# Selective scans in a two-layer MetaFormer: row sums at a unit's start, roots on GpSimd, whole-row products

## The chip, the cores and the metric

The kernel runs on one core of a Trainium2 chip. The metric is the device time of one execution in microseconds (us). Five engines work side by side, each through its own queue in order: PE (TensorE, matrix products), DVE (VectorE), ACT (ScalarE), POOL (GpSimd) and SP (SyncE, which here only issues transfers). They wait for one another by semaphores. SBUF is the on-chip memory of 128 partitions; PSUM holds the results of PE.

## The reference, cut to what matters

Two layers, each a mixing part and a feed-forward part with residuals, on x of shape (4, 256, 32, 32). The change lies in layer 1: its mixer is a selective scan in four directions, its feed-forward a router that sends each token to two of eight experts.

```python
def _selective_scan(x, A_log, D, W_delta, b_delta, W_B, W_C):
    delta = jax.nn.softplus(x @ W_delta + b_delta)
    Bm = x @ W_B
    Cm = x @ W_C
    A = -jnp.exp(A_log)
    dA = jnp.exp(delta[..., None] * A)
    dBx = (delta * x)[..., None] * Bm[:, :, None, :]
    def combine(left, right):
        a_l, b_l = left
        a_r, b_r = right
        return (a_l * a_r, a_r * b_l + b_r)
    _, h = jax.lax.associative_scan(combine, (dA, dBx), axis=1)
    y = jnp.einsum('blcn,bln->blc', h, Cm) + x * D
    return y
...
out1 = corr(flat)
out2 = jnp.flip(corr(jnp.flip(flat, axis=1)), axis=1)
rows = features.transpose(0, 2, 3, 1)
rows_f = jnp.flip(rows, axis=1).reshape(B, H * W, C)
out3 = jnp.flip(corr(rows_f).reshape(B, H, W, C), axis=1).reshape(B, H * W, C)
cols = features.transpose(0, 3, 2, 1)
cols_f = jnp.flip(cols, axis=1).reshape(B, W * H, C)
out4 = jnp.flip(corr(cols_f).reshape(B, W, H, C), axis=1)
...
mamba_out = (out1 + out2 + out3 + out4) / 4
...
# layer 1
x = x + _L1_conv_ref(_ln_c(x), ...)
t = _to_tokens(x)
t = t + _L1_ffn_ref(_ln_t(t), ...)   # normalizes again, then top 2 of 8 experts
```

Both norms before the experts divide by a root: `_ln_t` by sqrt(var + 1e-5), and the feed-forward's own by the root of the variance that is left, again with 1e-5.

## The kernel before

**Stages.** Layer 0 (attention with a top-k, its experts) takes the first 2190 us. Then the scan stage, 2192 to 3391 us, is written out by hand: instructions go to each engine's queue in the order in which the Python code issues them (`tc.manual_schedule()`). After it come the experts of layer 1 in 36 tiles of 256 slots, where a scheduler orders the instructions (the tail).

**A turn.** The scan stage has 128 units of work, called turns here: 4 batches b x 2 halves of channels c x 16 states s. Sixteen turns with one (b, c) make a unit. A turn works on tiles of 128 channels by 1024 positions in float32. In `turn(k)`, in this order:

- the generators in `steps` and `complete` are advanced by one step (called A in the prediction);
- PE: `begin()` clears the turn's sum in PSUM with a product of zeros (L2055), `columns_added()` adds the column scan of the turn before (L2095). If a generator uses the idle PSUM sum (`ps_m`), `begin` comes behind `columns_added`;
- ACT: `column_decays()` (da_c, L2033) for the next turn; POOL: `third()` of the turn before, an elementwise product into its da_c (L2084), which PE adds to the sum (L2061);
- PE: `output_added()` of two turns before adds yc to y (L2105);
- ACT: `products(cum)` for the next turn (L2037), from the row sums of delta, which are the same for all 16 turns of a unit;
- DVE: `forth()` (scan, L2066) and `back()` (scan into PSUM, L2073); POOL takes a small difference (gap, L2070); PE adds the forth scan twice (L2061);
- ACT: `decays()` (da, L2041); POOL and ACT: `inputs()` for the next turn (uu, L2049 and L2050); one scatter DMA if one is under way (L1984);
- DVE: `output()` of the turn before: yc = sum * C in two halves (L2101); then `come_in()`, a short scan (L2079);
- the generators are advanced by one more step (B);
- DVE: `cum`, the row sums, at the end of the turn two before a unit's first one (L2202), then `columns()`, the scan over columns (L2090).

So DVE's row in a bare turn is forth, back, yc, yc, come, columns.

**Generators beside the turns.** `Prep.steps` prepares the next batch (its norm, the products for B, C and delta, the softplus); it starts in turn 0 of batch 0's first unit, and in turn 8 of the first unit of batches 1 and 2. Its last pieces (L1861 to L1867), over four half rows, finish delta and dx and add D * x to the residual. `routed(b - 1)` starts in turn 2 of batches 1 to 3: `norm` (mean, transposes, squares on ACT, then two inverse roots) and `route` (best and second-best expert, counts, slots), after which 16 scatters go out, one a turn. For the last batch the same two generators run in the tail beside the experts' first tiles.

**The roots.** `rsqrt` (L1713) takes ACT's square root, which needs another function table than Exp, and refines its reciprocal by five small DVE instructions. `norm` does so twice.

Of the kernel before, what the change touches and what calls it, by code (L numbers as in the profile page):

```python
# [11 lines left out]
F32 = mybir.dt.float32  # L12
# [4 lines left out]
AF = mybir.ActivationFunctionType  # L17
ALU = mybir.AluOpType
# [16 lines left out]
E = 8  # L35
HID = 1024
NF = HID // P
NS = 16
# [24 lines left out]
def metaformer(ctx: ExitStack, tc: tile.TileContext, t: dict, out: bass.AP):  # L63
# [1530 lines left out]
    def route(b, tok, slot, space, psum, tag):  # L1594
# [15 lines left out]
        best(m1, hot1)  # L1610
        yield
        yield
        nc.vector.tensor_scalar(tok[:, :, C + 1], red, -1.0, float(E), ALU.mult, ALU.add)
        nc.vector.tensor_copy(tok[:, :, C], goal[:, ts(b, NT)])
# [63 lines left out]
    def norm(b, tok, pool, psum, tag, raw_tag, d):  # L1678
# [14 lines left out]
        for r in range(NT // 2):  # L1693
# [10 lines left out]
            for i in range(2):  # L1704
# [5 lines left out]
        ve, sd, r0, s1, s2 = (pool.tile([P, NT], F32, tag=f"nm_{i}", name=f"nm_{i}")  # L1710
                              for i in ("ve", "sd", "r0", "s1", "s2"))

        def rsqrt(dst):  # L1713

            yield
            nc.scalar.activation(sd, ve, AF.Sqrt)  # L1716
            yield
            nc.vector.reciprocal(r0, sd)
            nc.vector.tensor_tensor(sd, r0, r0, ALU.mult)
            nc.vector.tensor_tensor(sd, sd, ve, ALU.mult)  # L1720
            nc.vector.tensor_scalar(sd, sd, -0.5, 1.5, ALU.mult, ALU.add)
            nc.vector.tensor_tensor(dst, r0, sd, ALU.mult)

        nc.vector.tensor_scalar(ve, var, 1e-5, None, ALU.add)
        yield from rsqrt(s1)
        nc.vector.tensor_tensor(ve, s1, s1, ALU.mult)
        nc.vector.tensor_tensor(ve, ve, var, ALU.mult)
        nc.vector.tensor_scalar(ve, ve, 1e-5, None, ALU.add)
        nc.vector.tensor_tensor(lg1, lg1, s1.unsqueeze(2).to_broadcast([P, NT, E]), ALU.mult)
        yield from rsqrt(s2)  # L1730
        nc.vector.tensor_tensor(s2, s2, s1, ALU.mult)
# [37 lines left out]
    class Prep:  # L1769
# [7 lines left out]
        def steps(self, room, psum, tag):  # L1777
# [82 lines left out]
            for c, cols in parts:  # L1860
# [79 lines left out]
    with ExitStack() as st:  # L1940
# [21 lines left out]
        beside = [(2, places()), (FIRST, chain(whole(0), preps[0].steps(room, ps_n, "t"), lead.steps(preps[0]))), (SECOND, whole(1))]  # L1962
# [27 lines left out]
    with ExitStack() as st:  # L1990
# [22 lines left out]
        class Scan:  # L2013
# [84 lines left out]
            def output(self):  # L2098
                self.yc = [p2.tile([P, HALF], F32, tag="yc", name="yc", bufs=4) for h in range(NHALF)]
                for h in range(NHALF):  # L2100
                    nc.vector.tensor_tensor(self.yc[h], self.sum[:, ts(h, HALF)], self.cb[:, ts(h, HALF)], ALU.mult)  # L2101

            def output_added(self, y):
                for h in range(NHALF):
                    nc.tensor.matmul(y[:, ts(h, HALF)], ident, self.yc[h], start=(self.s == 0), stop=(self.s == NS - 1))  # L2105
# [31 lines left out]
        def turn(k):  # L2137
# [5 lines left out]
            next(complete, None)  # L2143
            shared = k > 0 and len(ps_m.left) < NHALF
# [20 lines left out]
            if 0 <= k < len(order):  # L2165
# [9 lines left out]
                if b + 1 < B and c * NS + s == (BEHIND if b > 0 else 0):  # L2175
                    steps.append(preps[b + 1].steps(room, ps_m, "hp"))
# [251 lines left out]
```

## Time and profile before

| what | us |
|---|---|
| median of 3 runs | 3993.39 (3991.88 to 3993.66) |
| profiled execution: its time | 3987.99 |
| profiled execution: its span | 3986.0 |
| scan stage, first forth to the last turn's end | 2192 to 3391 |
| busy in the span: PE, DVE, ACT, POOL | 3385.9, 3040.6, 2820.0, 1895.9 |
| scans on DVE (L2066, L2073, L2090), x128 each | 2.27 to 2.28 each |
| yc (L2101), x256 | 0.68 each |
| cum (L2202), x7 | 2.27 to 2.28 each |
| table loads for the norm's root (L1716), x8 | 1.28 each |

In the page, a row of engines shows the span in forty slices with the busy share in tenths. On a timeline, each row is a start, a duration, an engine, a source line, the operation, out<-in with shapes, and in brackets how long the engine was idle before it and what ended that. A table of windows gives, for stretches of time, the busy time of each engine, with the number of instructions, then the granted PE clock as a share of full speed, the share of the DMA engines and GB/s. Durations on one engine overlap a little[...].

### The profile page before, as it was taken

Reading aid. Unit: us, or ns where it says so; the run is one execution under the profiler, and the core shown is the slowest. Engines: PE = TensorE matmul, PEld = TensorE weight load, DVE = VectorE, ACT = ScalarE, POOL = GpSimd, SP = SyncE. Lnnn points to the kernel's source line nnn. Section 1 sums busy time; section 2 is a strip of 40 time slices with the busy share of each in tenths; the row PEclk is TensorE's granted clock in tenths of the full one; section 3 lists DMA queues with packets and bytes.
Section 4 is the critical chain, followed back from the end, with each engine's and each line's share of the span. In section 5 each row is a group of like instructions: output and inputs, shape, how many; then the busy total and the mean of one; then the engine's idle time right before and its main releaser. Section 6 shows DMA issues by size and latency. Waiting matters only on the chain. (4 is left out here: it accounts for less than half of the span.)

```text
span 3986.0 us, 49764 instructions
## 1 busy us (share of the span) xinstructions
PE 3385.9 (85%) x17283; PEld 1901.2 (48%) x17330; DVE 3040.6 (76%) x5416; ACT 2820.0 (71%) x3772; POOL 1895.9 (48%) x1643
## 2 busy tenths in 40 slices
PE   8368888888888888886697888988988989999996
PEld 5134444534354444543475333443433433788885
DVE  2689898998989898989476899999999999301112
ACT  2889999899989999996245677867767767322222
POOL 0145544575638475576343756545546546121111
PEclk8577887788778777787798999999999999999997
DMA  9400084000000000000374444334334334665555
GB/s 292 109 1 1 1 232 123 1 1 29 13 1 1 1 33 1 1 12 17 108 236 128 139 121 135 116 100 130 120 100 129 123 104 139 208 191 185 189 194 187
DMA packets 241815, 393.71 MB, mean 99 GB/s; under 512 B 31888, under 2 KB 182160, under 8 KB 241424
## 3 DMA queue, kind: packets, MB, share of 16 engines
q1 hardware_dynamic: 218016, 340.54, 27.7%
q0 software_dynamic: 19904, 48.48, 3.8%
q8 instruction: 139, 2.28, 0.2%
q10 hardware_dynamic: 3632, 1.40, 0.1%
q14 instruction: 124, 1.02, 0.1%
HBM read 280.41 MB, written 109.94 MB: 98 GB/s over the span
## 5 line engine op out<-in xcount | busy, mean ns | idle before, releaser
L823 POOL TENSOR_SCALAR dr<-s_n,last 128x1024 bf16<-128x1024 f32 x250 | 718.9, 2892 | 734.7 <-DVE state L851 407.8
L733 ACT ACTIVATE junk_a<-s_n,state 128x1024 int8<-128x1024 f32 x448 | 514.6, 1149 | 25.3 <-DVE state L857 9.0
L2084 POOL TENSOR_TENSOR da_c<-prod,come 128x1024 f32<-128x1024 f32 x128 | 248.3, 1940 | 444.8 <-DVE h L2090 353.5
L737 DVE TENSOR_SCALAR_CACHE_REDUCE junk_v<-s_n,state 128x1024 int8<-128x1024 f32 x320 | 408.6, 1277 | 8.8
L2276 ACT ACTIVATE hid<-hp,b 128x256 f32<-128x256 f32 x288 | 133.7, 473 | 357.0 <-PE hp L2274 356.8
L784 DVE SCALAR_TENSOR_TENSOR w<-s_n,win 128x1024 f32<-128x1024 f32 x256 | 350.9, 1371 | 5.3
L2095 PE MATMUL sum<-h,ident 128*128 128x512 f32 x512 | 269.1, 651 | 96.2 <-DVE h L2090 91.6
L787 DVE MAX8 win<-w 128x8 f32<-128x1024 f32 x256 | 314.5, 1228 | 8.8
L2073 DVE TENSOR_TENSOR_SCAN sum<-da,uu 128x1024 f32<-128x1024 f32 x127 | 289.7, 2281 | 27.2 <-remote 13.3
L891 ACT ACTIVATE ex<-sT 128x1024 f32<-128x1024 f32 x256 | 246.9, 1016 | 88.1 <-PE sT L883 88.1
L2049 POOL TENSOR_TENSOR uu<-dx,bb 128x1024 f32<-128x1024 f32 x127 | 302.4, 2381 | 1.9 <-DMA bb<-bc_d 1.8
L733 ACT ACTIVATE junk_a<-s_n,guess 128x1024 int8<-128x1024 f32 x256 | 294.2, 1149 | 7.2
L2066 DVE TENSOR_TENSOR_SCAN h<-da,uu 128x1024 f32<-128x1024 f32 x127 | 288.3, 2270 | 1.0 <-POOL uu L2049 1.0
L2090 DVE TENSOR_TENSOR_SCAN h<-da_c,uu 128x1024 f32<-128x1024 f32 x127 | 288.9, 2275 | 0.0
L901 PE MATMUL o_ps<-ex,vT 128*32 128x256 f32 x2048 | 238.5, 449 | 53.9 <-ACT ex L891 39.1
L2285 DVE TENSOR_TENSOR ys<-yp,b2e 128x512 f32<-128x512 f32 x36 | 24.9, 692 | 323.7 <-PE yp L2282 323.7
L2033 ACT ACTIVATE da_c<-delta,a_log 128x1024 f32<-128x1024 f32 x128 | 267.0, 2086 | 5.3 <-DMA rows_y<-ys 5.2
L2061 PE MATMUL sum<-da_c,ident 128*128 128x512 f32 x512 | 252.2, 615 | 16.0 <-POOL da_c L2084 10.3
L2287 POOL DMA_INDIRECT results<-ys,to x72 | 69.8, 969 | 411.8 <-DVE ys L2285 186.6
L2274 PE MATMUL hp<-xe,w 128*128 128x256 f32 x1152 | 260.2, 383 | 6.1 <-DVE xe L2262 5.9
L767 ACT COPY s_n<-sp 128x1024 f32<-128x1024 f32 x256 | 245.3, 1003 | 18.1 <-PE sp L759 10.3
L2282 PE MATMUL yp<-w2e,hid 128*128 128x256 f32 x1152 | 255.9, 379 | 0.0
(681 smaller groups left out, 7557.3 us busy)
## 6 DMA issues: line engine op xcount, KB each, us to landing
cb<-bc_d SPq DMA_DIRECT2D x128, 512.0 KB, 4.1
bb<-bc_d SPq DMA_DIRECT2D x127, 512.0 KB, 4.9
w<-in_w SPq DMA_DIRECT2D x36, 1024.0 KB, 5.1
w2e<-in_w SPq DMA_DIRECT2D x36, 1024.0 KB, 5.5
slots_x<-zeros SPq DMA_DIRECT2D x1, 33669.0 KB
slots_x<-zeros SPq DMA_DIRECT2D x1, 33282.0 KB, 120.9
w<-in_w SPq DMA_DIRECT2D x72, 256.0 KB, 3.1
xs<-slots_x SPq DMA_DIRECT2D x36, 261.0 KB, 3.3
```

Of the source, the lines that this page charges most:

```text
L733: nc.scalar.activation(junk, self.row(r), AF.Sign, bias=thr, scale=-1.0, accum_out=u)
L737: nc.vector.tensor_scalar(junk, self.row(r), thr, None, ALU.is_lt, ALU.add, accum_out=u)
L784: nc.vector.scalar_tensor_tensor(w, self.row(r), self.win[:, r, 0:1], self.row(r), ALU.is_gt if r < LAST_DVE else ALU.is_ge, ALU.subtract, ...
L787: nc.vector.max(out=self.win[:, r, 1:], in_=w)
L823: ins = eng.tensor_scalar(dr, self.row(r), self.last[:, r : r + 1], None, ALU.is_lt)
L2033: nc.scalar.activation(grid(self.da_c), cols_flipped(self.prep.delta[:, self.c]), AF.Exp, scale=self.decay)
L2049: nc.gpsimd.tensor_tensor(self.uu[:, 0], self.prep.dx[:, self.c], self.bb, ALU.mult)
L2066: nc.vector.tensor_tensor_scan(rows.rearrange("p r w -> p (r w)"), self.da, self.uu[:, 0], 0.0, ALU.mult, ALU.add)
L2073: nc.vector.tensor_tensor_scan(self.sum[:, ::-1], self.da[:, ::-1], self.uu[:, 0][:, ::-1], 0.0, ALU.mult, ALU.add)
L2090: nc.vector.tensor_tensor_scan(self.hs, self.da_c, self.uu[:, 1], 0.0, ALU.mult, ALU.add)
L2095: nc.tensor.matmul(cols_flipped(self.sum[:, ts(h, HALF)]), ident, grid(self.hs)[:, :, ts(h, half)], start=False, stop=False)
L2274: nc.tensor.matmul(hp[:, f % 2], self.w1[:, c, ts(f, P)], self.xe[:, c], start=(c == 0), stop=(c == CT - 1))
```

## The change: what it does

Five edits.

- `output()`: yc becomes one instruction over 1024 positions, into one buffer of two instead of two of four; the products that add it to y read its halves.
- `norm`: both inverse roots become a power of -1/2 on POOL, taken once each and not refined; seven small POOL instructions replace fifteen of DVE and two of ACT. The generator has two steps fewer. `minus_half` is a tile that layer 0's router has already.
- `route`: two small DVE writes (the expert's number and the token's goal) move two steps up, right behind the first search.
- `Prep.steps`: with `whole_rows`, the last pieces run over two whole rows of 1024 instead of four halves, so with half as many instructions and steps. The first preparation, which lies in layer 0's end, keeps the halves.
- `turn`: the row sums of a unit are taken in the turn before its first one, behind the A steps and before forth, instead of at the end of the turn before that, in front of `columns()`.

```diff
         best(m1, hot1)
+        nc.vector.tensor_scalar(tok[:, :, C + 1], red, -1.0, float(E), ALU.mult, ALU.add)
+        nc.vector.tensor_copy(tok[:, :, C], goal[:, ts(b, NT)])
         yield
         yield
-        nc.vector.tensor_scalar(tok[:, :, C + 1], red, -1.0, float(E), ALU.mult, ALU.add)
-        nc.vector.tensor_copy(tok[:, :, C], goal[:, ts(b, NT)])
         nc.vector.scalar_tensor_tensor(lg1, hot1, -1e30, lg1, ALU.mult, ALU.add)
...
-        def rsqrt(dst):
-
-            yield
-            nc.scalar.activation(sd, ve, AF.Sqrt)
-            yield
-            nc.vector.reciprocal(r0, sd)
-            nc.vector.tensor_tensor(sd, r0, r0, ALU.mult)
-            nc.vector.tensor_tensor(sd, sd, ve, ALU.mult)
-            nc.vector.tensor_scalar(sd, sd, -0.5, 1.5, ALU.mult, ALU.add)
-            nc.vector.tensor_tensor(dst, r0, sd, ALU.mult)
-
-        nc.vector.tensor_scalar(ve, var, 1e-5, None, ALU.add)
-        yield from rsqrt(s1)
-        nc.vector.tensor_tensor(ve, s1, s1, ALU.mult)
-        nc.vector.tensor_tensor(ve, ve, var, ALU.mult)
-        nc.vector.tensor_scalar(ve, ve, 1e-5, None, ALU.add)
+        nc.gpsimd.tensor_scalar(ve, var, 1e-5, None, ALU.add)
+        nc.gpsimd.tensor_tensor(s1, ve, minus_half, ALU.pow)
+        yield
+        yield
+        nc.gpsimd.tensor_tensor(ve, s1, s1, ALU.mult)
+        nc.gpsimd.tensor_tensor(ve, ve, var, ALU.mult)
+        nc.gpsimd.tensor_scalar(ve, ve, 1e-5, None, ALU.add)
+        nc.gpsimd.tensor_tensor(s2, ve, minus_half, ALU.pow)
+        nc.gpsimd.tensor_tensor(s2, s2, s1, ALU.mult)
         nc.vector.tensor_tensor(lg1, lg1, s1.unsqueeze(2).to_broadcast([P, NT, E]), ALU.mult)
-        yield from rsqrt(s2)
-        nc.vector.tensor_tensor(s2, s2, s1, ALU.mult)
         yield
...
-            for c, cols in parts:
+            for c, cols in [(c, slice(0, L)) for c in range(CT)] if whole_rows else parts:
                 dx = self.dx[:, c, cols]
...
             def output(self):
-                self.yc = [p2.tile([P, HALF], F32, tag="yc", name="yc", bufs=4) for h in range(NHALF)]
-                for h in range(NHALF):
-                    nc.vector.tensor_tensor(self.yc[h], self.sum[:, ts(h, HALF)], self.cb[:, ts(h, HALF)], ALU.mult)
+                self.yc = p2.tile([P, L], F32, tag="yc", name="yc")
+                nc.vector.tensor_tensor(self.yc, self.sum, self.cb, ALU.mult)
...
             next(complete, None)
+            if 0 < k + 1 < len(order) and order[k + 1][2] == 0:
+                b, c, _ = order[k + 1]
+                cum = p1.tile([P, L], F32, tag="cum", name="cum") if cum is lead.cum else lead.cum
+                nc.vector.tensor_tensor_scan(cum, inner, preps[b].delta[:, c], 0.0, ALU.mult, ALU.add)
...
-            if 0 <= k + 2 < len(order) and order[k + 2][2] == 0:
-
-                b, c, _ = order[k + 2]
-                if k < 0:
-                    cum = lead.cum
-                    return
-                cum = p1.tile([P, L], F32, tag="cum", name="cum") if cum is lead.cum else lead.cum
-                nc.vector.tensor_tensor_scan(cum, inner, preps[b].delta[:, c], 0.0, ALU.mult, ALU.add)
+            if k == -2:
+                cum = lead.cum
+                return
```

More of the change, by code (lines that the diff above doesn't have):

```diff
@@ L1709, in norm @@
             yield
-        ve, sd, r0, s1, s2 = (pool.tile([P, NT], F32, tag=f"nm_{i}", name=f"nm_{i}")
-                              for i in ("ve", "sd", "r0", "s1", "s2"))
-        def rsqrt(dst):
-            yield
-            nc.scalar.activation(sd, ve, AF.Sqrt)
-            yield
-            nc.vector.reciprocal(r0, sd)
-            nc.vector.tensor_tensor(sd, r0, r0, ALU.mult)
-            nc.vector.tensor_tensor(sd, sd, ve, ALU.mult)
-            nc.vector.tensor_scalar(sd, sd, -0.5, 1.5, ALU.mult, ALU.add)
-            nc.vector.tensor_tensor(dst, r0, sd, ALU.mult)
-        nc.vector.tensor_scalar(ve, var, 1e-5, None, ALU.add)
-        yield from rsqrt(s1)
-        nc.vector.tensor_tensor(ve, s1, s1, ALU.mult)
-        nc.vector.tensor_tensor(ve, ve, var, ALU.mult)
-        nc.vector.tensor_scalar(ve, ve, 1e-5, None, ALU.add)
+        ve, s1, s2 = (pool.tile([P, NT], F32, tag=f"nm_{i}", name=f"nm_{i}") for i in ("ve", "s1", "s2"))
+        nc.gpsimd.tensor_scalar(ve, var, 1e-5, None, ALU.add)
[7 more added lines that the diff above has]
+        nc.gpsimd.tensor_tensor(s2, s2, s1, ALU.mult)
         nc.vector.tensor_tensor(lg1, lg1, s1.unsqueeze(2).to_broadcast([P, NT, E]), ALU.mult)
-        yield from rsqrt(s2)
-        nc.vector.tensor_tensor(s2, s2, s1, ALU.mult)
         yield
@@ L1775, in __init__, with steps @@
             self.bc = bc_dram.tile([2 * NS, L], F32, tag="bc_d", name="bc_d")
-        def steps(self, room, psum, tag):
+        def steps(self, room, psum, tag, whole_rows):
             b = self.b
@@ L1960, in places @@
                     [P, *shape], F32, tag=f"at{len(shape)}", name="at", bufs=4))
-        beside = [(2, places()), (FIRST, chain(whole(0), preps[0].steps(room, ps_n, "t"), lead.steps(preps[0]))), (SECOND, whole(1))]
+        beside = [(2, places()), (FIRST, chain(whole(0), preps[0].steps(room, ps_n, "t", False), lead.steps(preps[0]))), (SECOND, whole(1))]
         for i in range(USUAL):
@@ L2098, in output @@
             def output(self):
-                self.yc = [p2.tile([P, HALF], F32, tag="yc", name="yc", bufs=4) for h in range(NHALF)]
-                for h in range(NHALF):
-                    nc.vector.tensor_tensor(self.yc[h], self.sum[:, ts(h, HALF)], self.cb[:, ts(h, HALF)], ALU.mult)
+                self.yc = p2.tile([P, L], F32, tag="yc", name="yc")
+                nc.vector.tensor_tensor(self.yc, self.sum, self.cb, ALU.mult)
             def output_added(self, y):
                 for h in range(NHALF):
-                    nc.tensor.matmul(y[:, ts(h, HALF)], ident, self.yc[h], start=(self.s == 0), stop=(self.s == NS - 1))
+                    nc.tensor.matmul(y[:, ts(h, HALF)], ident, self.yc[:, ts(h, HALF)], start=(self.s == 0), stop=(self.s == NS - 1))
             def finish(self, y):
@@ L2175, in turn @@
                 if b + 1 < B and c * NS + s == (BEHIND if b > 0 else 0):
-                    steps.append(preps[b + 1].steps(room, ps_m, "hp"))
+                    steps.append(preps[b + 1].steps(room, ps_m, "hp", True))
                 ys.append(ps_y.tile([P, L], F32, tag="y", name="y") if s == 0 else ys[-1])
```

## The prediction

> **What bounds the kernel now.** I read the page's slices first, then the scan stage (2192 to 3391 us, 128 turns) cut into its eight units of 16 turns, then single turns on the timeline. The columns of the second fence: stretch, its length, and busy time with instruction count of PE, PEld, DVE, ACT, POOL; then clock, DMA.
>
> ```profile
> DVE  2689898998989898989476899999999999301112
> ```
> ```profile
> 2342.00:2492.00 150.00, 128.64 (x305) 53.30 (x312) 145.29 (x116) 104.88 (x71) 96.11 (x63) 0.99 0.42 129
> 2492.00:2642.00 150.00, 138.89 (x391) 64.38 (x395) 139.84 (x163) 114.13 (x107) 69.06 (x46) 0.96 0.34 112
> ```
>
> DVE is full through the scans; a unit with a norm in it (the second row) has more DVE instructions, less DVE busy time and a lower clock. So the stage is DVE's row plus knots in the norm units. After it PE is full (tail, 3392 to 3890 us). One undisturbed turn on DVE:
>
> ```profile
> 3305.58 2.27 DVE L2066 TENSOR_TENSOR_SCAN h<-da,uu 128x1024 f32<-128x1024 f32 x1
> 3307.76 2.28 DVE L2073 TENSOR_TENSOR_SCAN sum<-da,uu 128x1024 f32<-128x1024 f32 x1
> 3309.94 1.27 DVE L2101 TENSOR_TENSOR yc<-sum,cb 128x512 f32<-128x512 f32 x2
> 3311.13 0.22 DVE L2079 TENSOR_TENSOR_SCAN come<-prod,gap 128x32 f32<-128x32 f32 x1
> 3311.26 2.27 DVE L2090 TENSOR_TENSOR_SCAN h<-da_c,uu 128x1024 f32<-128x1024 f32 x1
> ```
>
> Starts follow one another without a hole: 7.86 us a turn (next start 3313.44). What counts is the distance between starts, since ends overlap the next by 0.09 us. The two yc halves take 3309.94 to 3311.13. PE is nearly as full: 7.72 us busy of 7.80 in this turn.
>
> The knots. Before a unit's first scan the row sum (cum, L2202) sits between come and the column scan:
>
> ```profile
> 2792.42 0.60 PE L2055 MATMUL sum<-nought 128*128 128x512 bf16 x2
> 2795.15 3.68 PE L2095 MATMUL sum<-h,ident 128*128 128x512 f32 x4 [2.13 <-DVE h L2090]
> 2798.64 1.91 PE L2061 MATMUL sum<-da_c,ident 128*128 128x512 f32 x4
> ```
> ```profile
> 2800.58 1.29 DVE L2101 TENSOR_TENSOR yc<-sum,cb 128x512 f32<-128x512 f32 x2 [1.12 <-PE sum L2061]
> ```
>
> PE stood idle 2.13 us, its next four matmuls took 3.68 us instead of 1.98, and DVE then waited 1.12 us for the sum: the turn cost 9.09. yc's start also tells that it comes after all four adds of da_c (the last begins at 2799.95 and takes 0.59), not after the first half's two. The turns behind the seven cum scans, in windows (second-last but one number is the clock):
>
> ```profile
> 2488.70:2496.60 7.90, 7.68 (x18) 3.07 (x18) 7.90 (x8) 4.55 (x4) 4.49 (x3) 1.00 0.16 45
> 2795.00:2804.10 9.10, 8.95 (x17) 3.74 (x18) 7.98 (x7) 5.75 (x4) 5.48 (x4) 0.81 0.23 67
> 3102.30:3111.40 9.10, 8.92 (x17) 3.80 (x18) 8.01 (x7) 5.72 (x4) 5.48 (x4) 0.81 0.25 80
> ```
>
> At 2488 a PE gap of 2.35 us left the clock at 1.00: the drop is a matter of chance at gaps of 2 to 2.5 us. For the norm:
>
> ```profile
> 2574.03 1.28 ACT L1716 ACT_TABLE_LOAD   x1
> 2575.32 0.21 ACT L1716 ACTIVATE nm_sd<-nm_ve 128x8 f32<-128x8 f32 x1
> ```
> ```profile
> L304 POOL TENSOR_TENSOR space<-space,minus_half x3: 1670/1675/1683, 838.6 to 1720.2; 128x8 f32<-128x8 f32 x3
> ```
>
> The second is the layer-0 router's root, the operation that the norm will now use: 1.675 us on 128x8. Its neighbours L303 and L305 to L307 take 0.20 each.
>
> **What the Trainium skill says.** "TensorE: Matmul & The Clock Gate", Part 1 (What's actually happening): the clock falls to half after an idle window of about 3.4 us, and that window runs freely. The trace agrees on half rate (four matmuls 0.85 apart instead of 0.43) and on chance, but shows the drop after 2.13 us already. "VectorE: DVE Perf Modes", The TRN2 errata: an instruction pays a fixed cost on top of its elements. Agrees: 0.59 us between starts for 512 elements, 1.11 for 1024 (L2110, 2673.59 to 2674.70). "ScalarE: Activation LUTs", What ACT_TABLE_LOAD costs: 1283 ns; so does the trace. "GPSIMD Engine Reference", Specifications: it shares its SBUF interfaces with VectorE. The DVE scans take 2.27 with POOL's multiply beside them and without, so I charge nothing for POOL's added work.
>
> **The change part by part.** Turns are counted inside a unit, 0 to 15 for one (batch, half of channels); a step of a generator runs at the turn's start (A) or after come, ahead of the column scan (B).
>
> 1. Product with C over the whole row. One instruction of about 1.11 (L2110's distance; same size, one operand in PSUM) for a pair of 1.18: 0.07 x 128 = 9.0 us. Nothing starts later: yc already waits for all four adds. Its reader is the y matmul two turns on; two whole buffers hold what four halves held. If PE binds in the bare turns (7.72 of 7.80) some of it is lost: between -9 and -6. I take -9.0.
>
> 2. Roots on POOL. DVE loses per norm 8 dependent operations (2582.34 to 2583.84, 1.50 us), 6 more (2593.05 to 2594.15, 1.10) and L1724 (0.06): 2.66, three norms 8.0. One part is given back: with 1.5 us less work, the xm subtraction of turn 9 comes to its mean's matmul early, as it does in turn 8, where it waits 0.9 (column scan ends 2574.50, xm starts 2575.44); in the two norms with a preparation beside, +1.8. Sum -6.2. ACT loses four table loads and two roots a norm (5.5 us), but no DVE wait on ACT stands in the list of waits above 0.8 us: 0, at best -1. POOL gains 0.20 + 1.68 behind turn 8's uu and 4 x 0.20 + 1.68 behind turn 9's; it idles over 3.5 us there before da_c (3.5 busy of 10.7 in turn 9), and no DMA issue stands there in these turns: 0; uncovered it would cost at most 1.9 + 2.5 a norm.
>
> 3. The norm is two steps, so one turn, shorter, and routing follows a turn earlier, past the preparation's steps. The built order shows it: the counting matmuls move ahead of the next columns matmuls, and each scatter begins one turn earlier. Turn by turn (norm of unit 2, turns 8 to 17, 108.9 us now): turn 9 falls by the wait-corrected root; turn 12, where the second-best search (1.65) and the preparation's Newton steps (1.9) meet, gets 1.6 shorter; turn 10 and 13 carry the searches instead; a turn that begins its sum behind the columns matmuls appears at 13 (0.4 at full clock, 1.8 at half) and L1631's 1.2 us wait for PE goes. Net of the other parts about -0.8, twice, and -0.6 in the last: -2.2.
>
> 4. cum in front of the next forth instead of before columns. DVE work is the same; columns and POOL's da_c come 2.2 us earlier. PE then has columns, da_c and y matmuls (to 5.5 us after the column scan) before it waits for back at 6.6: a gap of 1.1, too short for the clock. prod, its reader on ACT, waits for da_c (2.05 after the column scan) as long as for cum (2.2). Saved: the excess of the seven turns behind over 7.86 and their own added operations: 0.8, 0, 1.2, 1.2, 1.25, 1.2, 1.9 = 7.6, less 0.8 which the preparation's own knots keep in two of them: -6.8.
>
> 5. Last pieces over whole rows, three preparations in the scans (the first is unchanged). First pair 0.70 + 0.61 twice becomes 1.24 + 1.14 (-0.24), second 0.58 + 0.66 twice becomes 1.12 + 1.20 (-0.18): 0.84 each, -2.5. But the eight turns with 1.3 us of it in B become four with 2.4 us. PE's gap there is 1.2 to 1.5 now; it becomes 2.3 to 2.6, the range where the clock sometimes falls. 12 turns x 0.5 x 1.2 = +7.2 (0 to 14.4). Sum +4.7.
>
> 6. The last norm stands in the tail, ordered by a scheduler. Four table loads (5.1 us) leave ACT, but PE is idle 0.2 us in 3440 to 3460: nothing to win. New: POOL's root stands behind the third results issue (3442.89 + 0.97), so s1 comes at about 3445.8 (3447.1 now); lg on DVE waits for it, the counting matmuls move up into the fourth tile's products, and the eight tok multiplies on ACT now lie between that tile's gelus. PE may wait up to 3 us there. +1.0 (0 to +3).
>
> Sum: -9.0 - 6.2 - 2.2 - 6.8 + 4.7 + 1.0 = -18.5. From the profiled execution (span 3986.0, time 3988.0) that is 3969.5; the median of the three runs stands 5.4 higher at 3993.4, so the time forecast is 3975 us.
>
> **Rivals.** (a) The clock does not fall behind the wider pieces and the norm units come loose entirely: part 5 is -2.5, parts 3 and 6 give 2 more: 3965. For it: gaps of 2.35 (2486.49 to 2488.85) and 2.40 (2381.55 to 2383.95) on PE's timeline left it high. (b) PE takes over: yc gives 6, all 12 piece turns fall to half clock (+7.2 over my half), the tail waits 3 and the norm units keep their knots (+2): 3993.4 - 18.5 + 3 + 7.2 + 2 + 2 = 3989, no change that a measurement can tell. For it: PE's 7.72 of 7.80. (c) Slower: the half clock becomes the rule. A slow group lasts 3.4 us and PE has no slack to recover, so it would spoil two turns, not one: 12 piece turns and 9 routing turns with over 1.6 us in B, 21 in all, at 1.7 each = 36 against savings without clock of 27: 4003. It decides from about 20 such turns (34 us). Against it: behind each of today's slow turns the next is normal. (d) The moved order isn't what the diff says: excluded by the built order.
>
> **Numbers.** Forecast case 0.66 (3965 to 3984), (a) 0.14, (b) 0.12, (c) 0.08. About 0.2% (8 us) is what a measurement tells from no change: faster 0.80, same 0.12, slower 0.08. Range 3957 to 3990: it leaves out (c), the upper half of (b) and the lowest part of (a).
>
> **What would show it.** Bare turns 7.79 long, one yc of about 1.20; seven turns behind cum at 7.8 with clock 1.00; no table load but the logarithm's and its return in the scans; POOL idle still ahead of da_c in turns 8 and 9; in the piece turns PE gaps of 2.3 to 2.6, half of them followed by 1.1 us waits of yc. The forecast is wrong if bare turns stay at 7.86, if the piece turns are all slow, or if DVE waits for nm_s of POOL.

## The result, and the profile after

The changed kernel takes 3976.84 us (median of 22 runs, 3965.81 to 3983.17); the kernel before takes 3986.11 beside it on the same chip (22 runs). The ratio is 0.9976 with a 95% interval of 0.9967 to 0.9985. The forecast of 3975, the range and the direction hold. The gain is 9.3 us, though, where the sum of the steps said 18.5, so half of that sum is missing.

The profiled executions fall into three stretches:

| stretch | before, us | after, us | difference | forecast |
|---|---|---|---|---|
| up to the first forth scan | 2191.86 | 2196.03 | +4.2 | 0 |
| scan stage, first forth (turn 0) to last forth (turn 127) | 1192.5 | 1178.0 | -14.5 | -19.5 |
| tail, from there to the end | 601.7 | 605.8 | +4.1 | +1.0 |

The change touches no instruction of the first stretch. It ended anywhere between 2179 and 2196 us in the profiles below, so I compare stage and tail and leave it out.

On the page, DVE's row looks as it did: full through the scans.

```profile
DVE  3589898998989898989476899999999999201112
```

The stage as one window shows more. Columns: stretch, length, busy time and instructions of PE, PEld, DVE, ACT, POOL, then clock, DMA share and GB/s. First the kernel before, then the changed one:

```profile
2191.86:3384.36 1192.50, 1072.13 (x2677) 459.37 (x2722) 1128.05 (x1093) 877.10 (x700) 669.14 (x458) 0.97 0.39 122
```
```profile
2196.03:3374.07 1178.04, 1077.38 (x2724) 460.86 (x2722) 1113.04 (x897) 861.41 (x682) 704.02 (x480) 0.97 0.38 123
```

DVE is the engine to read here, with busy time plus waiting making up the stage. Its busy time fell by 15.0 us. What is left of the length, its waiting, was 64.5 and is 65.0. The change took work off DVE and took no waiting away. Nor did it change the clock in sum: by the traces' clock record PE runs at half clock for 64.9 us of the stage before and for 64.8 us after. POOL's busy time rose by 35 us, although it was given only 21 small instructions for the roots of the three norms (some 13 us if each power took its 1.67). That is the trace's first hint of something the prediction left out.

A bare turn (116) on DVE's timeline:

```profile
3288.33 2.27 DVE L2055 TENSOR_TENSOR_SCAN h<-da,uu 128x1024 f32<-128x1024 f32 x1
...
3292.69 1.21 DVE L2089 TENSOR_TENSOR yc<-sum,cb 128x1024 f32<-128x1024 f32 x1
3293.82 0.22 DVE L2068 TENSOR_TENSOR_SCAN come<-prod,gap 128x32 f32<-128x32 f32 x1
...
3296.13 2.27 DVE L2055 TENSOR_TENSOR_SCAN h<-da,uu 128x1024 f32<-128x1024 f32 x1
```

From forth to forth it is 7.80 us, and it was 7.86; yc to come is 1.13, and was 1.19. Up to here the forecast holds. Now a unit's beginning (turns 63 and 64), where the row sum cum is new; DVE, POOL and PE of the timeline:

```profile
2792.16 2.27 DVE L2135 TENSOR_TENSOR_SCAN lead_cum<-inner,delta 128x1024 f32<-128x1024 f32 x1
...
2792.41 3.73 POOL L2073 TENSOR_TENSOR da_c<-prod,come 128x1024 f32<-128x1024 f32 x1 [1.91 <-DVE h L2079]
...
2796.19 2.72 PE L2050 MATMUL sum<-da_c,ident 128*128 128x512 f32 x4 [1.90 <-POOL da_c L2073]
```

POOL's product takes 1.91 in nearly every turn, and 3.73 here, where it starts just behind cum. It ends 1.7 us after cum does, as if it had stood waiting until cum was done. PE, which needs the product, idles 1.90 where the prediction counted 1.1, and its four matmuls behind that gap take 2.72 instead of 1.98: the clock fell there as it did before. Five of the seven cum scans look like this. In the other two the product came first, and cum is the one that is stretched (turn 47):

```profile
2642.00 1.91 POOL L2073 TENSOR_TENSOR da_c<-prod,come 128x1024 f32<-128x1024 f32 x1 [4.32 <-DVE h L2079]
...
2642.95 3.11 DVE L2135 TENSOR_TENSOR_SCAN cum<-inner,delta 128x1024 f32<-128x1024 f32 x1
...
2650.49 2.06 PE L2050 MATMUL sum<-h,twice 128*128 128x512 f32 x2 [2.72 <-DVE sum L2062]
```

After a PE gap of 2.72 the two matmuls take 2.06 instead of 1.02: half clock. The same stretching stands in the norm (turn 105), where the second power on POOL began 0.13 us behind a column scan:

```profile
3189.81 2.29 DVE L2079 TENSOR_TENSOR_SCAN h<-da_c,uu 128x1024 f32<-128x1024 f32 x1
...
3189.94 3.63 POOL L1718 TENSOR_TENSOR nm_s<-nm_ve,minus_half 128x8 f32<-128x8 f32 x1
...
3193.80 1.91 POOL L2073 TENSOR_TENSOR da_c<-prod,come 128x1024 f32<-128x1024 f32 x1
...
3197.79 1.23 DVE L2089 TENSOR_TENSOR yc<-sum,cb 128x1024 f32<-128x1024 f32 x1 [1.32 <-PE sum L2050]
```

The power took 3.63 instead of 1.67 in all three norms of the scans. It held back da_c, PE's addition of it, and here DVE's yc. In the tail there is a wait of another kind:

```profile
3433.13 1.67 POOL L1712 TENSOR_TENSOR nm_s<-nm_ve,minus_half 128x8 f32<-128x8 f32 x1
3435.81 1.67 POOL L1718 TENSOR_TENSOR nm_s<-nm_ve,minus_half 128x8 f32<-128x8 f32 x1
...
3437.82 0.51 ACT L1723 ACTIVATE tok<-tok,nm_s 128x256 f32<-128x256 f32 x1 [4.60 <-POOL nm_s L1719]
...
3438.74 1.85 PE L2261 MATMUL hp<-xe,w 128*128 128x256 f32 x4 [3.45 <-ACT hid L2263]
```

The two powers are not stretched, but they follow one another, and ACT's first token multiply waits 4.60 us for the second. Behind it in ACT's queue stands a gelu of an expert tile, and PE waits 3.45 us for that.

### The profile page after: what moved, and what is told of

The parts are those of the page before. It is cut to its first block, busy times and chain, and to the rows that moved or that the text cites. A ratio compares the mean times of both kernels' runs of the same rounds, so it can differ in the third digit from the quotient of the medians.

```text
span 3979.8 us, 49680 instructions
## 1 busy us (share of the span) xinstructions
PE 3387.3 (85%) x17330; PEld 1898.6 (48%) x17330; DVE 3024.2 (76%) x5204; ACT 2799.2 (70%) x3748; POOL 1934.2 (49%) x1671
## 3 DMA queue, kind: packets, MB, share of 16 engines
q8 instruction: 139, 2.28, 0.2%
## 5 line engine op out<-in xcount | busy, mean ns | idle before, releaser
L2073 POOL TENSOR_TENSOR da_c<-prod,come 128x1024 f32<-128x1024 f32 x128 | 256.6, 2005 | 389.3 <-DVE h L2079 333.7
L2050 PE MATMUL sum<-h,twice 128*128 128x512 f32 x512 | 248.0, 607 | 12.0 <-DVE sum L2062 12.0
```

What stands on the lines that cost most here:

```text
L2050: nc.tensor.matmul(self.sum[:, ts(h, HALF)], ident if eye is None else eye, view[:, ts(h, HW // NHALF), :], start=False, stop=last)
```

## The experiments

My theory was: POOL and DVE exclude each other while a DVE instruction reads two operands from SBUF, as the column scan and cum do; forth and back, whose da lies in PSUM, do not. That, and not the clock, would be what the prediction missed. The rivals were that the stretched instructions are chance and harmless, and that the clock ate the gain. All kernels start from the changed one. For the stage I give DVE's busy time and its waiting (length less busy).

**Extra POOL work beside the column scan.**

```diff
+                if k in (116, 119, 122):
+                    extra = room("xm", [CT, L])[:, 0]
+                    come, prod = scans[k].come, scans[k].prod[:, :HW, :]
+                    if k == 116:
+                        nc.gpsimd.tensor_tensor(grid(extra), prod, come.unsqueeze(2).to_broadcast([P, HW, HW]), ALU.mult)
+                    elif k == 119:
+                        nc.gpsimd.tensor_scalar(grid(extra), prod, come[:, 0:1], None, ALU.mult)
+                    else:
+                        nc.gpsimd.tensor_tensor(extra[:, :8], come[:, :8], come[:, 8:16], ALU.mult)
```

> Three extra POOL instructions with results that nobody reads, each started by come, so together with the column scan: in turn 116 a product of 128x1024 with two SBUF operands (the form of da_c), in turn 119 a one-operand multiply by a column of 128x1024, in turn 122 a product of 128x8. Theory (exclusion with a DVE scan of two SBUF operands): in turn 116 either POOL's 1.91 becomes 3.7 to 4.2 or the column scan's 2.27 becomes 3.1 to 4.2; the 128x8 product takes about 2.2 to 2.5 instead of 0.20. The one-operand multiply tells whether POOL's count of operands matters: it is stretched by about 2 too if POOL's one access is enough, and not at all if two are needed. Rival (a long POOL instruction is only a late end of something it waits for): all keep their usual 1.91 and 0.20 and the column scan 2.27.

POOL's timeline of turns 116, 119 and 122:

```profile
3285.17 3.42 POOL L2188 TENSOR_TENSOR xm<-prod,come 128x1024 f32<-128x1024 f32 x1
...
3309.98 4.35 POOL L2190 TENSOR_SCALAR xm<-prod,come 128x1024 f32<-128x1024 f32 x1
...
3336.89 1.73 POOL L2192 TENSOR_TENSOR xm<-come 128x8 f32<-128x8 f32 x1
```

The column scans of these turns start at 3284.62, 3309.40 and 3336.36, and the next forth follows each by 2.18 or 2.19, undisturbed. The first POOL product ends 1.7 us after its scan, so nearly all of its 1.91 came behind it. The small one, 0.20 elsewhere, ends at 3338.62, with the scan (3338.63). Both began under such a scan and got nowhere until it was about over. The small one had begun some 0.55 us late, behind a DMA issue on POOL, which is why 1.73 is less than I expected. The one-operand multiply ends 2.7 us after its scan, but its own length was not measured, so whether it was held is not shown. The rival, a late end of something waited for, is out: all three had their operands.

**Which DVE instructions exclude.**

```diff
+                if k in (116, 120, 124):
+                    spare = room("xm", [CT, L])
+                    come, prod = scans[k].come, scans[k].prod[:, :HW, :]
+                    nc.gpsimd.tensor_tensor(grid(spare[:, 0]), prod, come.unsqueeze(2).to_broadcast([P, HW, HW]), ALU.mult)
+                    for _ in range(3):
+                        if k == 116:
+                            nc.vector.tensor_scalar(spare[:, 1], cum, come[:, 0:1], None, ALU.mult)
+                        elif k == 120:
+                            nc.vector.tensor_tensor(spare[:, 1], cum, inner, ALU.mult)
+                        else:
+                            nc.vector.tensor_tensor(spare[:, 1], scans[k + 1].da, inner, ALU.mult)
```

> Extra work with results that nobody reads, ahead of the column scan, on both engines at once: POOL multiplies 128x1024 (the form of da_c, two SBUF operands, 1.91 us by itself) while DVE runs three instructions of 128x1024 in a row: in turn 116 a multiply by a column (one SBUF operand), in turn 120 a product of two SBUF operands, in turn 124 a product of one PSUM and one SBUF operand. Theory (what excludes POOL is a DVE instruction with two operands in SBUF, of any kind): POOL's extra product takes 1.91 in turns 116 and 124 and, in turn 120, either 3 us or more itself or the DVE product beside it is stretched by over 1 us. Rival (it is scans that exclude POOL): POOL's product takes 1.91 in all three and DVE's products keep their usual length, about 1.2.

The three kinds as groups by source line; after the count come shortest, median and longest in ns:

```profile
L2190 DVE TENSOR_SCALAR xm<-cum,come x3: 753/861/2282, 3280.2 to 3283.5; 128x1024 f32<-128x1024 f32 x3
```
```profile
L2192 DVE TENSOR_TENSOR xm<-cum,inner x3: 1201/1225/2819, 3317.7 to 3321.8; 128x1024 f32<-128x1024 f32 x3
```
```profile
L2194 DVE TENSOR_TENSOR xm<-da,inner x3: 1224/1224/1225, 3356.0 to 3358.5; 128x1024 f32<-128x1024 f32 x3
```

With one operand in PSUM nothing happens: three times 1.22, and POOL's product took 1.93. With two in SBUF, one DVE product is stretched to 2.82 and POOL's took 2.42. So it is the place of the operands and not the scan; the two engines take turns, instruction by instruction. The theory was too narrow on one point: a multiply of one SBUF operand by a column, which takes 0.75 us where the product takes 1.20, is stretched to 2.28 as well, and POOL's product beside it took 2.23. The Trainium skill, "GPSIMD Engine Reference", Specifications, says just this: contention with DVE instructions that have two SBUF inputs or run in a two-port performance mode. That the multiply ran in such a mode is not in the trace; only its shorter time speaks for it. The prediction had read the page and set it aside, because scans beside POOL's product showed nothing. The only scans that ran beside it in the kernel before were those with an operand in PSUM.

**cum back in its old place.**

```diff
-            if 0 < k + 1 < len(order) and order[k + 1][2] == 0:
-                b, c, _ = order[k + 1]
-                cum = p1.tile([P, L], F32, tag="cum", name="cum") if cum is lead.cum else lead.cum
-                nc.vector.tensor_tensor_scan(cum, inner, preps[b].delta[:, c], 0.0, ALU.mult, ALU.add)
...
+            if 0 <= k + 2 < len(order) and order[k + 2][2] == 0:
+
+                b, c, _ = order[k + 2]
+                cum = p1.tile([P, L], F32, tag="cum", name="cum") if cum is lead.cum else lead.cum
+                nc.vector.tensor_tensor_scan(cum, inner, preps[b].delta[:, c], 0.0, ALU.mult, ALU.add)
```

> Only the row sum cum goes back to its old place, ahead of the column scan. Theory (a DVE instruction with both operands in SBUF and a POOL instruction exclude each other, so the new place has its own price): no da_c product on POOL longer than 2.0 us at a unit's beginning, but PE idles 2.1 to 2.4 us there again and turns behind cum cost up to 9.1 (turns 63, 95); the stage grows by 2 to 5 us over the changed kernel's 1178.0, less than the 6.8 that the prediction gave to this part. Rival (the stretched products of the new place are chance or belong to the norm, and the move is worth what was forecast): the stage grows by 6 to 8 us.

The stage as a window, and PE at turn 63:

```profile
2180.77:3354.31 1173.54, 1069.93 (x2724) 457.54 (x2722) 1110.83 (x898) 861.24 (x682) 694.07 (x480) 0.98 0.40 124
```
```profile
2779.21 1.98 PE L2084 MATMUL sum<-h,ident 128*128 128x512 f32 x4 [2.06 <-DVE h L2079]
```

Both theory and rival expected the stage to grow, and it fell by 4.5 us. The stretched instructions are gone: 10 us less on POOL, and 1.6 less on the seven cum scans of DVE (all 2.26 to 2.29 again). The gap of 2.06 us is there, but the matmuls behind it take 1.98, full clock; in the kernel before, a gap of 2.13 at this spot was followed by half clock. What tells the two gaps apart is shown under the next run. Taken over the seven beginnings alone (three turns each), the old place is 0.9 us better; the other 3.6 us lie in turns without it, above all 1, 17 and 87, whose clock came out differently. In two kernels that change nothing in these 21 turns (the extra DVE work above, and the old roots in the tail below), the clock alone moves their sum by -1.5 and +2.7 us. So 0.9 us shows neither a gain nor a loss of the move; what is shown is that nothing like 6.8 came back.

**The same kernel again, unaltered.**

> The changed kernel unaltered, once more. It leaves nothing out. Theory (which gap of about 2 us is followed by half clock is decided by when it falls): DVE's busy time is 1113.0 within 0.5, while single turns differ from the first profile by 0.4 to 1.7 us at gaps of 1.9 to 2.5 us, and the stage differs from 1178.0 by up to 5. Rival (the clock follows the program alone): every turn is within 0.1 of the first profile.

The differences that I expected did not come. DVE's busy time is the same, the stage is 1177.8, and every turn is within 0.11 us of the first profile. The extra-POOL kernel repeats turns 0 to 115 within 0.04. But the kernels with an edit in the tail only (old roots, below) and with the extra DVE work, whose scan stage has the same instructions as the changed kernel up to turn 115, differ from it by 1.2 to 1.7 us in single turns (16, 17, 76, 77 and 112 in the first).

The traces' clock record says why, and it bears the theory out. In all fourteen profiles every rise and fall of PE's clock lies on a grid of 3.413 us, and in the stage half clock lasts one or two steps of the grid (3.41 or 6.83 us). What PE did in one step tells the clock of the next. The kernel with cum apart (below) has a gap of 2.06 us in turn 63 and one of 2.07 in turn 65. Here each row is one step of the grid; PE's busy time comes right after the length, and the clock is the third number from the end. First turn 63:

```profile
2780.05:2783.46 3.41, 2.52 (x7) 0.77 (x5) 3.41 (x4) 3.41 (x3) 0.59 (x1) 1.00 0.63 161
2783.46:2786.87 3.41, 2.16 (x5) 0.86 (x6) 3.41 (x3) 0.72 (x2) 1.94 (x2) 1.00 0.46 185
2786.87:2790.29 3.42, 3.42 (x9) 1.51 (x10) 3.42 (x4) 2.26 (x3) 3.29 (x3) 1.00 0.00 0
```

Then turn 65:

```profile
2807.35:2810.77 3.42, 1.35 (x5) 0.43 (x4) 3.42 (x3) 2.21 (x2) 0.48 (x1) 1.00 0.80 252
2810.77:2814.18 3.41, 3.41 (x6) 1.33 (x5) 3.41 (x3) 1.15 (x1) 2.08 (x3) 0.50 0.00 0
```

In turn 63 the gap (2782.57 to 2784.63) lies across the boundary of two steps, and both keep over 2 us of work. In turn 65 the gap (2808.13 to 2810.20) lies within one step and leaves 1.35 us of work there; the next step runs at half clock. I counted the steps at full clock in the stages of the fourteen profiles. All 119 in which PE was busy for less than 40% were followed by half clock, and so were 30 of the 48 between 40 and 45%. Above 45% it was 30 of 4423, all of them in turns 42, 43, 74 and 75, where the mean matmuls of a preparation's norm fill the step. So the drop is not a matter of chance, as the prediction had it: it depends on where a gap falls in the grid.

The repeat had the grid at nearly the same place, 0.32 us behind the first forth where the first profile had 0.52 (and the extra-POOL kernel 0.56). In the two kernels that differ it stood at 0.69 and 3.33. A single turn's 1.2 us, or 3 us of a stage, are therefore not put down to an edit unless it lies in that edit's own turns, and even there one profile has the clock's luck in it.

**yc in halves again.**

```diff
-                self.yc = p2.tile([P, L], F32, tag="yc", name="yc")
-                nc.vector.tensor_tensor(self.yc, self.sum, self.cb, ALU.mult)
+                self.yc = [p2.tile([P, HALF], F32, tag="yc", name="yc", bufs=4) for h in range(NHALF)]
+                for h in range(NHALF):
+                    nc.vector.tensor_tensor(self.yc[h], self.sum[:, ts(h, HALF)], self.cb[:, ts(h, HALF)], ALU.mult)
```

> Only the product with C goes back to two halves. Theory (DVE's row sets the bare turns): a bare turn grows from 7.795 to 7.86 us and the scan stage from the first forth to the last (1178.0 us in the changed kernel) grows by 0.065 x 128 = 8.3 us. Rival (PE's 7.72 of 7.80 binds, and yc only moved the wait): the bare turn stays within 0.02 of 7.795 and the stage within 3 us.

```profile
2188.10:3370.55 1182.45, 1077.23 (x2724) 458.45 (x2722) 1121.02 (x1023) 861.48 (x682) 703.87 (x480) 0.98 0.40 123
```

DVE's busy time rises by 8.0 us and the stage by 4.4, between theory and rival. Turn by turn both are right, in different places: 79 turns grow by 0.05 to 0.08, about thirty by less than 0.05 and most of those not at all, and 14 turns move with the clock (-1.0 in all). Among the turns that don't grow are 8, 9, 12, 38, 70 and 102, with a norm or a preparation beside them, where back waits 0.7 to 1.4 us for PE. There DVE gets to that wait earlier and stands longer.

**The old roots in the scans, and then in the tail.** The changed norm stands on one side of a condition on the batch, the old one on the other; for the tail the condition is `b == B - 1`:

```diff
+        if b < B - 1:
...
+            nc.vector.tensor_scalar(ve, var, 1e-5, None, ALU.add)
+            yield from rsqrt(s1)
...
+        else:
...
             nc.gpsimd.tensor_tensor(s1, ve, minus_half, ALU.pow)
```

> The changed kernel with square root on ACT and reciprocal on DVE again in the three norms inside the scans (so their routing also starts a turn later again); the tail keeps POOL's power. Theory (DVE's row is busy time plus waits for PE, and the roots took 7.9 us of busy time off it): DVE's busy time in the stage rises by 7 to 8.5 us from 1113.0, its idle time stays between 58 and 68, and the stage comes out at 1182 to 1189. Rival (the norm turns are set by PE's routing matmuls or by ACT's table loads): the stage moves by less than 3 us, or by more than 12.

```profile
2183.79:3362.58 1178.79, 1074.62 (x2724) 458.83 (x2722) 1118.93 (x943) 877.53 (x700) 678.85 (x458) 0.98 0.39 123
```

Busy time rises by 5.9, less than I expected, and the stage by only 0.75. By turns: the norm's own (34 to 48, 66 to 80, 98 to 113) grow by 4.4, 1.4 and 0.7, in sum 6.5 us (in the two kernels that change nothing there, the clock moves the turns of one norm by up to 1.6). The rest falls by 5.8, most of it in turns 1, 15, 17, 55 and 87, which hold no step of a norm: the shift of the clock's pattern again. By the stage's number the rival (less than 3 us) came true, though these shifts stand against the norms' 6.5 us in it.

> Only the last norm, which stands in the tail, gets its roots by square root on ACT and reciprocal on DVE again; the norms inside the scans keep POOL's power. Theory (POOL's roots stand behind the third results issue and delay the token multiplies, which stand between the gelus): PE's idle of 3.45 us ahead of hp near 3438 disappears, and the time from the last forth to the end shrinks by about 4 us to what it was in the kernel before; the scan stage stays within 0.5 us of 1178.0. Rival (the tail's 4 us are chance of clock and DMA): the tail changes by less than 1.5 us or PE idles as long elsewhere.

The tail falls to 602.5, by 3.25 us. PE's timeline at the place of the 3.45 us gap:

```profile
3429.49 4.48 PE L2285 MATMUL hp<-xe,w 128*128 128x256 f32 x20
3433.81 0.59 PE L2293 MATMUL yp<-w2e,hid 128*128 128x256 f32 x2
```

PE goes on without a hole. The tail's loss is POOL's roots. The stage grew by 1.15, more than the 0.5 allowed, with no changed instruction in it.

**One power a norm.**

```diff
+        both = pool.tile([P, 2, NT], F32, tag="nm_both", name="nm_both")
+        nc.gpsimd.tensor_scalar(both[:, 0], var, 1e-5, None, ALU.add)
+        nc.gpsimd.tensor_scalar(both[:, 1], var, 1.0 + 1e-5, 1e-10, ALU.mult, ALU.add)
+        nc.gpsimd.tensor_tensor(both, both, minus_half.unsqueeze(1).to_broadcast([P, 2, NT]), ALU.pow)
+        s1, s2 = both[:, 0], both[:, 1]
```

> The changed kernel with one power a norm instead of two: since s1*s1 is 1/(var+eps), the second root times the first is (var*(1+eps)+eps*eps)^-0.5, which does not need the first; both stand in one 128x16 tile. The first power ran ahead of the column scan in the scans' norms (1.67 us), the second behind its start (3.63 us). Theory (exclusion): without the second group da_c is no longer pushed back by 1.7 us, turn 106 falls from 11.04 to about 9, turns 41 and 73 by up to 1.5, the stage by 3 to 6 us; in the tail PE's idle of 3.45 us ahead of hp shrinks by about 2.7 (the second group's time on POOL). Rival (POOL has room in these turns, as the prediction said, and the slow power costs nothing): the stage stays within 1 us of 1178.0.

```profile
3421.25 2.94 POOL L1713 TENSOR_TENSOR nm_both<-nm_both,minus_half 128x16 f32<-128x16 f32 x1
...
3425.55 1.13 PE L2258 MATMUL hp<-xe,w 128*128 128x256 f32 x4 [2.40 <-ACT hid L2260]
```

The stage falls by 5.7 us, but the theory earns only a part of it. Turn 106 falls by 1.44, to 9.6 where about 9 was expected; turns 41 and 73 don't move, so there the stretched power cost nothing; the rest is the clock's pattern. The power takes 2.94 for 16 columns against 1.67 for 8, so most of it goes by the column, and the tail's gap shrinks by 1.05 only; the tail as a whole did not get shorter (606.3).

**Last pieces in halves again** (`True` to `False` in the call of `Prep.steps`).

> The changed kernel with the preparation's last pieces in halves again. The changed kernel's whole-row pieces gave turns 54 to 61 and 86 to 93 0.2 us each and took 0.8 in turns 14 to 21, with three of the twelve turns at half clock. Theory (gap of 1.2 to 1.5 us with halves keeps the clock, and the rows' saving is 0.84 a preparation): turns 54 to 61 and 86 to 93 are each within 0.4 us of the changed kernel's, none at half clock, and the stage lies between -2 and +3 of 1178.0. Rival (the pieces' clock drops are what ate the forecast gain): the stage falls by 4 us or more.

The stage falls by 3.3 us, between the two. The pieces' own turns give 1.7, 0.3 and 0.3 in the three preparations. In the changed kernel three of the twelve whole-row turns were slow (17, 55, 87); PE in turn 55:

```profile
2721.66 3.27 PE L2084 MATMUL sum<-h,ident 128*128 128x512 f32 x4 [2.25 <-DVE h L2079]
```

With halves all three run at full clock, which is worth 1.2 each, and the added instructions cost 0.77 a preparation on DVE. But all three run at full clock with whole rows too, in the kernels with one power and with the old roots in the scans, where the grid stood elsewhere: there the pieces' turns are 4.8 and 4.9 us shorter than in the changed kernel. Which form is better is not settled by one profile each.

**cum apart from other work.** The old place, and for a unit of the same batch already in the second turn of the unit before:

```diff
+            if k >= 0 and (k % (CT * NS) == 1 or k % (CT * NS) == CT * NS - 2) and k + 2 < len(order):
+                unit = k // NS + 1
+                b, c, _ = order[unit * NS]
+                cums[unit] = p1.tile([P, L], F32, tag="cum", name="cum") if unit % 2 else lead.cum
+                nc.vector.tensor_tensor_scan(cums[unit], inner, preps[b].delta[:, c], 0.0, ALU.mult, ALU.add)
```

> The changed kernel with cum ahead of the column scan as before, but, where the next unit has the same batch (turns 15, 47, 79, 111 behind it), already in the second turn of the unit, where no piece of the norm or the preparation runs; the other three stay in the unit's second-last turn. Theory (at the old place cum costs only its own 2.18 us and a gap of 2.06 us on PE, which leaves the clock up; the knots of turns 46 to 48 and 78 to 80 come of cum and routing in one turn): against e2_cum_old_place (1173.5) the stage falls by 3 to 6 us, against the changed kernel (1178.0) by 7 to 10. Rival (the clock falls by chance at each gap over 2 us wherever it is): turns 1, 33, 65, 97 become 1 us longer than 7.79 + 2.18 and the stage is within 2 us of 1173.5.

The rival's stage came true: it is 1173.7. Turns 46 and 48 lose 3.0 and 1.7 us, but turn 33 gains cum's 2.18 and turn 34 another 1.3 at half clock, and so it is at 65 and 97, after PE gaps of 2.07. At 31, 63 and 95 the same gap left the clock up, because it lay across a boundary of the grid; at 33, 65 and 97 it lay within one step, or all but 0.05 us of it.

> One power a norm and cum apart, together, with the product with C and the pieces of the changed kernel. If the two act in different turns, their stage gains add: 1178.0 less 10 to 15 us, 1163 to 1168, and with 2 us less in the tail a time of 3960 to 3968 on average, 0.995 of the kernel before. Rival (the turns of the norm are set by another wait, which takes the place of both): less than 8 us of stage.

Stage 1172.3: the totals don't add. In the edits' own turns they do: turn 106 falls by 1.44 as with one power, and turns 46 and 48 by 3.0 and 1.7 as with cum apart. What is missing lies in other turns, where the clock's pattern differs among the three profiles. The time is 3964.6 us, 0.9946 of the kernel before (0.9927 to 0.9966).

**Everything in small portions.** One power in the scans, the old roots in the tail, cum in halves where the batch is the same, whole-row pieces with one operation a turn:

```diff
+            at = k % (CT * NS)
...
+                for cols in ([slice(0, L)] if at > 1 else [ts(at, HALF)]):
+                    nc.vector.tensor_tensor_scan(cums[unit][:, cols], inner[:, cols], preps[b].delta[:, c, cols], 0.0,
+                                                 ALU.mult, ALU.add)
...
                 nc.vector.tensor_tensor(dx, dx, v[:, c, cols], ALU.add)
+                if whole_rows:
+                    yield
+                    yield
```

> What the runs so far point to, in one kernel: product with C over the whole row; one power a norm in the scans and the old roots in the tail; cum for a unit of the same batch in two halves of the row, in the first two turns of the unit before; the last pieces over whole rows, but one operation a turn instead of two. Theory (DVE work in portions of about 1.1 us ahead of the column scan keeps PE's gap below 1.8 us, where the clock hardly ever fell: 14 of 243 gaps in the runs so far, against 46 of 196 from 1.8 to 2.35): busy time as in e8_power_and_cum (1110), idle time 62 less 3 to 6, stage 1166 to 1170, the tail 602 to 603 as in e4_tail_old_roots, and the time 0.993 of the kernel before, 3955 to 3960. Rival (the idle time belongs to PE's own matmuls in norm and preparation turns): idle stays at 60 to 65 and the stage at 1171 to 1175.

```profile
2179.09:3348.83 1169.74, 1070.92 (x2724) 456.23 (x2722) 1109.75 (x902) 860.52 (x682) 682.92 (x468) 0.98 0.39 124
```

The stage is 1169.7, the tail 602.3 and the time 3959.3 us (six runs), 0.9945 of the kernel before (0.9926 to 0.9964). That interval lies just below the changed kernel's 0.9967 to 0.9985, so this version beats both; against the one before it the ratio is no better, though stage and tail are 2.6 and 3.9 us shorter. Stage, tail and time came out as the theory said (the ratio did not quite: 0.993 was expected), but not in its way. Waiting is 60.0, at the rival's edge, 2 us less than 62, and it is as low (59.9 to 60.6) in three kernels above without smaller portions. That the portions removed waiting is not shown. Of the 60.0, 31.6 are back standing for PE, nearly all in turns with a norm or a preparation beside them, where PE has matmuls of its own to add.

## Why the prediction was right in its total and wrong in its sum

That the time came out 1.8 us from the forecast is luck. Two things met: the stage and the tail fell short by 8 us together, and the kernel before, timed beside it, was itself 7 below the three runs that the forecast was set to. The steps, one by one:

1. *yc over the whole row, -9.0.* The mechanism is right. DVE's busy time on yc fell by 7.6 (0.060 a turn, not 0.07). Of this about 5.4 reached the stage in the undoing run (4.4, and 1.0 that its clock hid). The prediction's own bound (-6 if PE binds) was the better value: it looked at PE's share in bare turns, where DVE still decides, while PE decides in about thirty others.
2. and 3. *Roots and routing, -8.4 together.* Undoing them costs 6.5 us in the norm's own turns. DVE's row lost what was counted: the 45 instructions were 6.75 us of busy time, and 8.0 with the small holes between dependent ones. What failed is "it idles over 3.5 us there before da_c", priced at 0. POOL idles there while DVE's column scan is running, and that is when it cannot work. The price was 1.44 at turn 106 and nothing at 41 and 73, less than the "at most 1.9 + 2.5 a norm" that the prediction named.
4. *cum ahead of forth, -6.8.* This is the step that failed. "A gap of 1.1" was 1.90 at turns 31, 63, 95 and 111 and 2.72 at 47 and 79, since cum and da_c ran one after the other; the seven cum scans cost DVE 1.6 us more. The term that it put at nothing is POOL's da_c beside a scan of two SBUF operands: 3.73 us where it counted 1.91. The gap is also not "too short for the clock": behind it the matmuls of turn 63 slow down again, so that turns 63 and 64 together gained 0.6 us where 1.2 was forecast, and turns 31 and 32 lost 0.6. What the move is worth in all stays open within the clock's luck; in the undoing run, where the gaps at 63 and 95 lay across the grid's boundaries, these turns are 0.9 us better without the move.
5. *Pieces over whole rows, +4.7.* The work is right (-2.4 on DVE against -2.5). Three of twelve turns were slow instead of six. Against halves the pieces cost 2.3 us in their own turns in one pair of profiles; in two others with whole rows none of the three was slow.
6. *The tail, +1.0 (0 to +3).* Right place and right mechanism ("the eight tok multiplies on ACT now lie between that tile's gelus"), but 4.1 measured and 3.25 by undoing: PE's wait was 3.45, beyond the end given.

Of the signs it named, the bare turn and yc came true; "seven turns behind cum at 7.8 with clock 1.00" and "POOL idle still ahead of da_c" did not. Of its signs of being wrong, DVE's wait for nm_s showed once, 3.57 us in the tail. In hindsight the forecast of -19.5 for the stage was just DVE's removed work (9.0 + 8.0 + 2.5), since its gains and losses in waiting cancelled. The measured 14.5 is DVE's removed work too, with 0.5 more waiting: 7.6 + 6.75 + 2.4, less cum's 1.6, makes 15.2 beside the 15.0.

What stays open: undoing the parts one at a time accounts, in their own turns, for 5.4 + 6.5 - 0.9 - 2.3 = 8.7 of the 14.5 us. The other 5.8 belong to no part that I could single out, and each of these sums has the clock's luck of 1 to 3 us in it. Why the grid stood at nearly the same place in the repeat, and why the clock also falls behind steps full of a preparation's mean matmuls, was not settled either.

## What to carry to other kernels

Before moving work to POOL, or DVE work next to POOL's, look at where each operand of the DVE instructions beside it lies: idle time of POOL under a DVE instruction with two SBUF operands is not free time. A row of the profile in which POOL waits for just that instruction can't show it; look for the same POOL instruction at two lengths, and at what DVE ran beside each. The length alone is no proof: in turns 9, 10, 23 and 24 of both kernels, behind the issue of gathers on POOL, da_c takes 2.51 to 2.52 us though only scans with an operand in PSUM run beside it. An edit that moves a gap of PE can't be priced by the gap's length alone; where it falls in the clock's grid decides, so one profile of each kernel isn't enough. Split a stage into the bound engine's busy time and its waiting before pricing an edit: busy time added up reliably here (-15.0 measured of -19.5, each foreseen term within 1.5), while the waiting stayed at 60 to 66 us in every kernel that had no extra work.

## What the runs showed of the hardware that I had not expected

- DVE and POOL take turns, by whole instructions. Behind a scan that reads two SBUF operands, POOL's 1.91 becomes 3.42 to 3.74 and a 128x8 product of 0.20 becomes 1.73; behind POOL's product the scan's 2.27 becomes 3.11. A one-operand DVE multiply of SBUF data at 0.75 us a 128x1024 does it too. One operand in PSUM: no effect (1.22 and 1.93).
- POOL's power costs 1.67 us for 128x8 and 2.94 for 128x16.
- PE's clock is set step by step on a grid of 3.413 us, by what PE did in the step before. Less than 40% busy was always followed by half clock (119 of 119 steps), more than 45% never, but for 30 steps with a preparation's mean matmuls. So a gap of 1.90 us within a step brought the clock down (turn 63), and one of 3.35 us across a boundary left it up (turn 111 with cum in its old place: 1.72 and 1.75 us of work in its two steps). The Trainium skill, "TensorE: Matmul & The Clock Gate", Part 1, tells of a window of about 3.4 us that runs freely; the grid agrees in length, and its place differed from profile to profile. The page has the clock fall after an idle window, and here a window that was busy for up to 40% was enough.
